# Spreading the closings, loads and weighings over the last stage of a two-layer graph-attention kernel

## The chip, the cores and the metric

The kernel runs on one core of one Trainium2 chip. The metric is the device time of one execution in microseconds (us), lower is better. The kernel before takes 3591.52 us, the median of three runs that lie between 3589.25 and 3591.77 us.

## The reference

The input `x` is 8 batches of 2048 nodes with 256 features; `adj` is one symmetric 2048 x 2048 adjacency matrix. Layer 0 is an attention with 4 heads of 64 features whose softmax runs over chunks of 256 keys, followed by two layer norms. Layer 1 is a graph attention with the same 4 heads:

```python
Wh = (h @ W).reshape(B, N, 4, 64)
e = s_src[:, :, None, :] + s_dst[:, None, :, :]      # per head
e = where(e > 0, e, 0.2 * e);  e = where(adj != 0, e, -inf)
alpha = softmax(e, axis=2)
h_out = elu(einsum('bijh,bjhd->bihd', alpha, Wh))
x = layernorm(x + h_out)                              # the output
```

The change touches layer 1 of the last batch, and what is done beside it, alone.

## The kernel before, in words

**Layer 1 in factored form.** The exponential of a sum is a product, so the weight of a pair of nodes is the maximum of a row value and a column value `gd`, masked, and the column's own factor `ed` is multiplied into the values beforehand. `waug` is the tile with the values of one batch: 128 partitions x 16 node tiles x 4 heads x 65 columns (64 values and the factor for the denominator). `factors(b, sd, waug)` makes these: its step `rows` stores the row factors to DRAM (`rowD`) and then has GpSimd (POOL in the profile) multiply `waug` by `ed` head by head, four `tensor_mul` in a row at line 767, the "weighing".

**Tiles and units.** Layer 1 of one batch is 8 units `(m, h)`: half `m` of the rows (1024 rows, 8 blocks of 128) and head `h`, in the order m=0 with h=0..3, then m=1 with h=0..3. A unit has 16 tiles, one for each block of 128 columns; all together are 128 tiles. One tile is one 128 x 1024 array `e` and then 32 small matmuls of TensorE (PE) at line 915 that accumulate `e` against `waug[:, j, h, :]` into the banks `pa`.

**The last stage stands alone.** Layer 1 of batch b is normally worked off beside layer 0 of batch b+1. The last batch, b = 7, has nothing beside it: `Layer1.alone` is true, and the program ends with a loop of 64 slots, two tiles each, so 8 slots make one unit. The order of instructions is written out by hand and every engine works through its own queue in that order; semaphores tie the queues together. In this stage

- VectorE (DVE) makes two tiles of three, at line 886, from a row `rowp` that ScalarE (ACT) has copied ("lifted") into PSUM at line 826;
- every third tile (`by_pool`) is made ahead by ACT (Relu and Identity, lines 855 and 856) and POOL (multiplication with the mask, line 857). `make_ahead` keeps four tiles (`LEAD`) ahead of the tile at hand;
- the row of a unit comes by four DMAs of the SP queue (`load_row`, posted in quarters, line 220 in the profile). It is asked for at tile 8 of the unit before (line 867) and lifted at tile 12 (line 879);
- the masks come as two tiles `et`, one for each half `m`, each by four DMAs of 512 KB (`load_masks`, line 799): the first before the stage, the second in `begin()` right ahead of it, into the buffer that the `waug` of batch 6 had;
- when a unit ends, ACT copies `pa` into `sums` (line 927), and a generator `close` finishes it in five steps, one step a slot (`rest(1)` in `step`): a denominator and its reciprocal `dn` on DVE (lines 940, 941), a multiplication on POOL (945), Exp and Relu on ACT (956, 957), and the sum into `h1` on DVE (959).

**Closings.** `Close` is the last layer norm of a group of 512 nodes. It loads `x1` of the group by four DMAs of 128 KB (`load`), adds it to `h1` on POOL (`pool`, line 997, 128 x 1024 elements), takes the statistics on DVE (`stats`, lines 540 to 549) with a power and a product on POOL (550, 551), and applies them on ACT (`finish`, line 588). The stores to the output follow with the next `send()`, on the SP queue as well. Tables say in which slot which group has which step: `CLOSING_ALONE` for the four groups of batch 6, `ENDING` for batch 7, whose groups 2 and 3 are finished after the loop. The slot's order is `send()`, then `lower.step()`, then the closings' steps.

Before the loop the remaining tiles of batch 6 are worked off; their DVE instructions read the row `srow` from SBUF, not from PSUM. The last tile of batch 6 and the first of batch 7 follow each other on PE without a barrier.

Of the kernel before, what the change touches and what calls it, by code (L numbers as in the profile page):

```python
# [10 lines left out]
F8 = mybir.dt.float8e4  # L11
# [6 lines left out]
P = 128  # L18
# [4 lines left out]
def adj_resnorm_kernel(  # L23
# [19 lines left out]
    nc = tc.nc  # L43
    B, N, F = x.shape
    H, D = a_src.shape
    NT = N // P
    NCH = N // CH
# [8 lines left out]
    QT = CH // P  # L56
# [15 lines left out]
    UNITS = [(m, h) for m in range(len(BANKS)) for h in range(H)]  # L72
# [4 lines left out]
    WIDE = max(BANKS)  # L77
    AHEAD_E = 5
    LEAD = 4
# [40 lines left out]
    qT = big.tile([P, KC, N], F32, tag="qT", name="qT")  # L120
    kT = big.tile([P, KC, N], F32, tag="kT", name="kT")
# [4 lines left out]
    edgeD = [tc.dram_tile([P, NT, n * P], F8, name=f"edgeD{m}") for m, n in enumerate(BANKS)]  # L126
# [79 lines left out]
    def send():  # L206
        while outgoing:
            outgoing.pop(0)()
# [4 lines left out]
    def drip(n=1):  # L213
        while pieces and n:
            pieces.pop(0)[1]()
            n -= 1
# [7 lines left out]
    def need(key):  # L224

        at = [k for k, piece in enumerate(pieces) if piece[0] == key]
        if at:
            drip(at[-1] + 1)
# [492 lines left out]
    def factors(b, sd, waug):  # L721

        s, d = sd[:, :H, :], sd[:, H:, :]
        top = small.tile([P, H], F32, tag="top", name="top")
        topb = top.unsqueeze(2).to_broadcast([P, H, NT])
        ed = small.tile([P, H, NT], F32, tag="ed", name="ed", bufs=1)
        gd = small.tile([P, H, NT], F32, tag="gd", name="gd")
        st = {}  # L730
        banks = one_bank if b + 1 < B else two_banks

        def most():
            nc.vector.tensor_reduce(top, d, AX.X, ALU.max)
            pt = banks([P, CH], "pt")
            nc.tensor.transpose(pt[:H, :P], top, identf)
            st["most"] = small.tile([H, 1], F32, tag="most", name="most")
            nc.vector.tensor_reduce(st["most"], pt[:H, :P], AX.X, ALU.max)

        def spread():  # L740
            pb = banks([P, CH], "pb")
            nc.tensor.matmul(
                pb[:, :H],
                lhsT=st["most"].to_broadcast([H, P]),
                rhs=identf[:H, :H],
                start=True,
                stop=True,
            )
            nc.vector.tensor_copy(top, pb[:, :H])
            nc.vector.tensor_add(s, s, topb)  # L750
            nc.vector.tensor_scalar(s, s, FAR, None, ALU.min)
            nc.scalar.activation(s, s, AF.Exp, scale=1.0 - SLOPE)
            nc.vector.tensor_sub(d, d, topb)
            nc.vector.tensor_scalar(d, d, -FAR, None, ALU.max)
            nc.scalar.activation(ed, d, AF.Exp)
            nc.scalar.activation(gd, d, AF.Exp, scale=SLOPE - 1.0)

        def rows():

            pr = banks([P, CH], "pr1")  # L760
            nc.tensor.transpose(pr[: H * NT, :P], s.rearrange("p h t -> p (h t)"), identf)
            flat = small.tile([H * NT, P], F32, tag="flat", name="flat", bufs=1)
            nc.scalar.copy(flat, pr[: H * NT, :P])
            nc.scalar.dma_start(out=rowD[b].rearrange("h (t p) -> (h t) p", p=P), in_=flat)
            nc.gpsimd.tensor_copy(waug[:, :, :, D], ed.rearrange("p h t -> p t h"))
            for h in range(H):
                nc.gpsimd.tensor_mul(
                    waug[:, :, h, :D],
                    waug[:, :, h, :D],
                    ed[:, h, :].unsqueeze(2).to_broadcast([P, NT, D]),  # L770
                )

        return gd, [most, spread, rows]


    class Layer1:
# [17 lines left out]
        def load_masks(self, m):  # L794

            pool, tag = ((big, "vaug"), (blocks, "waug"))[m]
            t = pool.tile([P, NT, WIDE * P], F8, tag=tag, name="et")
            for j in range(0, NT, QT):
                nc.sync.dma_start(out=t[:, j : j + QT, :], in_=edgeD[m][:, j : j + QT, :])
            self.masks[m] = t  # L800

        def start(self):
            self.load_row(0)
# [56 lines left out]
        def make(self):  # L860

            if self.made == TILES:
                return
            k = self.made
            n, j = k // NT, k % NT
            _, h = UNITS[n]
            if j == NT // 2:
                self.load_row(n + 1)
            self.made += 1
            if not self.alone:  # L870
                drip()
                if j == 0:
                    need(("row", self.b, n))
                self.load_edge(k + AHEAD_E)
                pool, tag = self.room
                e = pool.tile([P, WIDE * P], F32, tag=tag, name="e")
                row = self.rows[n]
            else:
                if j == NT - LEAD:
                    self.lift(n + 1)  # L880
                self.make_ahead(k)
                if self.by_pool(k):
                    return
                e = prp.tile([P, WIDE * P], F32, tag="pr", name="e")
                row = self.lifted[n]
            nc.vector.scalar_tensor_tensor(  # L886
                e,
                row,
                self.gd[:, h, j : j + 1],
                self.mask(k),  # L890
                op0=ALU.max,
                op1=ALU.mult,
            )
            self.e[k] = e
# [40 lines left out]
        def close(self, u, raw):  # L935
            m, h = UNITS[u]
            n = BANKS[m]

            dn = small.tile([P, n, 1], F32, tag="dn", name="dn")
            nc.vector.tensor_scalar(dn, raw[:, :, D:D1], 1e-30, None, ALU.max)  # L940
            nc.vector.reciprocal(dn, dn)
            yield 1
            if self.alone:
                v = raw[:, :, :D]
                nc.gpsimd.tensor_mul(v, v, dn.to_broadcast([P, n, D]))
            for k in range(n):
                if k == n // 2:
                    yield 1
                if not self.alone:
                    v = raw[:, k, :D]  # L950
                    nc.scalar.activation(v, v, AF.Copy, scale=dn[:, k, :])  # L951
            yield 1

            ee = small.tile([P, n, D], F32, tag="ee", name="ee")
            hp = raw[:, :, :D]
            nc.scalar.activation(ee, hp, AF.Exp)
            nc.scalar.activation(hp, hp, AF.Relu)
            yield 1
            nc.vector.scalar_tensor_tensor(
                h1[:, FIRST[m] : FIRST[m] + n, h * D : (h + 1) * D],  # L960
                ee,
                1.0,
                hp,
                op0=ALU.min,
                op1=ALU.add,
            )

        def step(self):
            self.rest(1)
            for _ in range(STEP):  # L970
                self.make()
                self.use()
# [117 lines left out]
    for g in range(NCH):  # L1090
# [36 lines left out]
        11: [(3, "factors"), (3, "finish")],  # L1127
    }
    CLOSING_ALONE = {
        -1: [(g, "load", kT, g) for g in range(NCH)],  # L1130
        1: [(0, "pool")],
        2: [(1, "pool")],
        3: [(0, "stats")],
        4: [(1, "stats")],
        5: [(0, "finish")],
        6: [(1, "finish")],
        8: [(2, "pool")],
        9: [(3, "pool")],
        10: [(2, "stats")],
        11: [(3, "stats")],  # L1140
        12: [(2, "finish")],
        13: [(3, "finish")],
    }
    ENDING = {
        30: [(g, "load", qT, g) for g in range(NCH)],
        37: [(0, "pool")],
        38: [(1, "pool")],
        39: [(0, "stats")],
        40: [(1, "stats")],
        41: [(0, "finish")],  # L1150
        42: [(1, "finish")],
        61: [(2, "most")],
        62: [(3, "most")],
    }
    lower = None
    for b in range(B):
        waug = blocks.tile([P, NT, H, D1], F32, tag="waug", name="waug")
        sd = small.tile([P, 2 * H, NT], F32, tag="sd", name="sd", bufs=1)
        closing = Closing(b - 2, CLOSING) if b > 1 else None
# [111 lines left out]
        send()  # L1271
        before = group
        gd, fs = factors(b, sd, waug)
        group = None

# [68 lines left out]
        lower = coming  # L1344
# [2 lines left out]
        lower.tail += undone  # L1347

    closing, ending = Closing(B - 2, CLOSING_ALONE), Closing(B - 1, ENDING)
    closing.do(-1, "load")  # L1350
    for _ in range(STEP):
        lower.make()
    for s in range(SLOTS):
        send()
        lower.step()
        for each in (closing, ending):
            each.do(s, "load", "pool", "stats", "most", "finish")
    send()
# [46 lines left out]
```

## Time and profile before

| what | value |
|---|---|
| median of three runs | 3591.52 us (3589.25 to 3591.77) |
| the profiled execution's own time | 3592.51 us |
| its span, from first to last instruction | 3590.6 us |
| busy over the span | PE 3512.4 us (98%), DVE 3040.5 (85%), ACT 2302.9 (64%), POOL 1424.7 (40%) |
| last stage, first to last tile on PE | about 3417.4 to 3577.3 us of the span |
| after the last tile | 13 us to the end of the span |

The profile is of one execution. "Busy" is the time in which an engine has an instruction under way; a wait is named by the engine that waits, the line, and what released it. PEclk is the share of TensorE's full clock that was granted. SPq is the queue of SyncE, which only issues DMAs. The last stage is 4.5% of the span, so the shares of the whole page say little of it; its own windows have to be asked for.

### The profile page before, as it was taken

The numbers are of one execution on the slowest core, as the hardware profiler recorded it, in microseconds if no ns is written. First come the engines' busy times: TensorE is split into PE (matmuls) and PEld (weight loads), VectorE is DVE, ScalarE is ACT, GpSimd is POOL, SyncE is SP. The second block draws the span as 40 slices with busy tenths as digits, with TensorE's granted clock in tenths as the row PEclk, the third lists the DMA queues.
The fourth block names the chain that finished last, engine by engine and source line by source line (L and its number), as shares of the span: only waits on it lengthen the run. The fifth ranks groups of instructions, "written<-read, shape, count | busy, mean of one in ns | idle before, by whom it ended". The sixth has DMA issues, their size and how long they took to land.

```text
span 3590.6 us, 170172 instructions
## 1 busy us (share of the span) xinstructions
PE 3512.4 (98%) x76892; PEld 2619.9 (73%) x76892; DVE 3040.5 (85%) x3655; ACT 2302.9 (64%) x4120; POOL 1424.7 (40%) x1255
## 2 busy tenths in 40 slices
PE   8999999999999999999999999999999999999787
PEld 5666677777777777776777767777677777777687
DVE  5886699977999699996999969998699987998787
ACT  5787556656666567665666657666576655666476
POOL 1555233333434333333443324334243333443366
PEclk9999999999999999999999999999999999999888
DMA  7663333443444444443444434444443443443341
GB/s 178 151 132 81 82 101 101 109 102 106 117 107 104 91 122 116 109 104 86 123 108 110 102 96 126 107 107 96 106 126 106 109 100 101 118 108 95 95 126 38
DMA packets 719848, 386.06 MB, mean 108 GB/s; under 512 B 433040, under 2 KB 679184, under 8 KB 719120
## 3 DMA queue, kind: packets, MB, share of 16 engines
q1 hardware_dynamic: 669120, 341.48, 38.0%
q10 hardware_dynamic: 50000, 33.70, 3.0%
q8 instruction: 601, 9.85, 1.2%
q14 instruction: 127, 1.04, 0.1%
HBM read 318.11 MB, written 56.89 MB: 104 GB/s over the span
## 4 chain that ended last, share of the span: by engine, by line
PE 86%; DVE 7%; issue 2%; DMA 2%; ACT 1%; POOL 1%; SPq 0%; DVEq 0%; ACTq 0%; POOLq 0%
PE pa L915 24%; PE pc L473 23%; PE ps L422 23%; PE pp L366 6%; PE po L625 3%; PE pv L382 3%; PE pw L667 3%; DVE e L886 3%; DVE pr L439 2%; POOL acc L499 1%; DMA et<-edgeD 1%; DVE h L439 0%; POOL part L497 0%; ACT e L855 0%; PE pm L270 0%
## 5 line engine op out<-in xcount | busy, mean ns | idle before, releaser
L462 ACT ACTIVATE pr<-pr 128x1024 f32<-128x1024 f32 x960 | 996.7, 1054 | 438.7 <-DVE pr L439 364.8
L439 DVE SCALAR_TENSOR_TENSOR pr<-ps,slab 128x1024 f32<-128x1024 f32 x960 | 1115.3, 1203 | 101.3 <-PE ps L422 83.6
L886 DVE SCALAR_TENSOR_TENSOR e<-srow,gd,et 128x1024 f32<-128x1024 f32 x896 | 1170.7, 1340 | 5.2
L915 PEld LDWEIGHTS pa<-waug,e 128*64 128x64 f32 x32768 | 1014.2, 140 | 213.4 <-issue 168.9
L915 PE MATMUL pa<-waug,e 128*64 128x65 f32 x32768 | 1066.6, 225 | 35.3 <-DVE e L886 30.7
L473 PE MATMUL pc<-vaug,pr 128*64 128x65 f32 x30720 | 980.8, 222 | 6.4 <-DVE pr L439 6.0
L497 POOL TENSOR_TENSOR part<-raw,rd 128x512 f32<-128x512 f32 x446 | 473.7, 1062 | 1221.3 <-DVE rd L490 1217.2
L473 PEld LDWEIGHTS pc<-vaug,pr 128*64 128x64 f32 x30720 | 938.0, 138 | 22.2 <-DVE pr L439 18.9
L422 PE MATMUL ps<-qT,kT 64*64 64x512 f32 x8192 | 942.3, 596 | 5.5 <-DVE pr L439 3.2
L422 PEld LDWEIGHTS ps<-qT,kT 64*64 64x64 f32 x8192 | 287.3, 132 | 482.5 <-issue 270.1
L480 ACT COPY raw<-pc 128x520 f32<-128x520 f32 x512 | 303.0, 592 | 492.7 <-PE pc L473 490.0
L499 POOL TENSOR_TENSOR acc<-acc,part 128x512 f32<-128x512 f32 x446 | 583.9, 1309 | 35.1
L490 DVE RECIPROCAL rd<-raw 128x8 f32<-128x8 f32 x512 | 100.4, 196 | 130.2 <-ACT raw L480 122.9
L497 POOL TENSOR_TENSOR acc<-raw,rd 128x512 f32<-128x512 f32 x64 | 66.8, 1044 | 361.1 <-DVE rd L490 361.1
L667 PE MATMUL pw<-w_sb,x1T 128*64 128x264 f32 (+1 forms) x800 | 124.4, 391 | 0.4 <-issue 0.2
L625 PE MATMUL po<-wo_sb,qT 128*64 128x256 f32 (+1 forms) x912 | 122.3, 384 | 0.1
L366 PE MATMUL pp<-xT,wk_sb 128*128 128x512 f32 x256 | 118.4, 603 | 2.9 <-DVE xT L322 1.6
L366 PE MATMUL pp<-xT,wq_sb 128*128 128x512 f32 x256 | 117.4, 598 | 0.0
L951 ACT ACTIVATE sums<-sums,dn 128x64 f32<-128x64 f32 x448 | 117.2, 334 | 0.0
L382 PE MATMUL pv<-wv_sb,xT 128*128 128x256 f32 x512 | 116.6, 381 | 0.0
L382 PEld LDWEIGHTS pv<-wv_sb,xT 128*128 128x128 f32 x512 | 95.9, 190 | 20.2 <-issue 7.2
L886 DVE SCALAR_TENSOR_TENSOR e<-rowp,gd,et 128x1024 f32<-128x1024 f32 x86 | 103.9, 1270 | 0.8 <-ACT rowp L826 0.8
(142 smaller groups left out, 2511.6 us busy)
## 6 DMA issues: line engine op xcount, KB each, us to landing
et<-edgeD SPq DMA_DIRECT2D x896, 128.0 KB, 2.8
slab<-clipD SPq DMA_DIRECT2D x256, 256.0 KB, 3.8
srow<-rowD SPq DMA_DIRECT2D x256, 128.0 KB, 3.6
xg<-in_x_dram SPq DMA_DIRECT2D x128, 128.0 KB, 3.3
x1D<-y ACTq DMA_DIRECT2D x32, 512.0 KB, 3.1
ctxD<-acc ACTq DMA_DIRECT2D x56, 256.0 KB, 3.6
ctx<-ctxD SPq DMA_DIRECT2D x224, 64.0 KB, 3.0
xp<-in_x_dram SPq DMA_DIRECT2D x224, 64.0 KB, 2.4
```

The source lines that it names most:

```text
L366: nc.tensor.matmul(pps[c], lhsT=w[:, kc, c * P : (c + 1) * P], rhs=st["xT"][:, kc, :], start=(kc == 0), stop=(kc == KC - 1),)
L382: nc.tensor.matmul(pv[:, u, :], lhsT=st["xT"][:, kc, u * P : (u + 1) * P], rhs=wv_sb[:, kc, :], start=(kc == 0), stop=(kc == KC - 1),)
L422: nc.tensor.matmul(ps[z * D : (z + 1) * D, k, :], lhsT=kT[rows, hp, t * P + z * D : t * P + (z + 1) * D], rhs=qT[rows, hp, cols], start=Tr ...
L439: nc.vector.scalar_tensor_tensor(pr, ps, -CLIP, row.unsqueeze(1).to_broadcast([P, 2, CH]), op0=ALU.max, op1=ALU.min,)
L462: nc.scalar.activation(pr, pr, AF.Exp, scale=0.125)
L473: nc.tensor.matmul(pc[z * D : (z + 1) * D, k, to], lhsT=probs[s][u][:, k, i * P + z * D : i * P + (z + 1) * D], rhs=vaug[:, KT * c + u, 2 ...
L480: nc.scalar.copy(raws[s].rearrange("p k i d -> p k (i d)"), pc[:, :, : QT * D1])
L497: engine.tensor_mul(part, raw[:, :, :, :D], rd.to_broadcast([P, 2, QT, D]))
L499: engine.tensor_add(accv, accv, part)
L667: nc.tensor.matmul(pw[z, k, : F + 2 * H], lhsT=self.x1T[:, c, u * P + z.start : u * P + z.stop], rhs=w1_sb[:, c, :], start=(c == 0), stop= ...
L886: nc.vector.scalar_tensor_tensor(e, row, self.gd[:, h, j : j + 1], self.mask(k), op0=ALU.max, op1=ALU.mult,)
L915: nc.tensor.matmul(self.pa[i // QT][z * D : (z + 1) * D, i % QT, :], lhsT=e[:, i * P + z * D : i * P + (z + 1) * D], rhs=self.waug[:, j, h ...
```

## The change

In layer 1 of the last batch:

- the weighing of heads 1, 2 and 3 is taken out of `rows` and done in slots 1, 5 and 9 of the loop; head 0 is still weighed in `rows`;
- the second mask's four DMAs move from `begin()` to slots 15, 17, 19 and 21, one in each;
- a unit's row is asked for at tile 1 of the unit before in place of tile 8, and lifted at tile 8 in place of tile 12;
- `x1` of a group of batch 6 is loaded in slots 0, 2, 9 and 12 in place of all four ahead of the loop; for batch 7 in slots 34, 36, 45 and 47 in place of all at 30;
- the steps of the closings lie further apart: `pool` of batch 6 in slots 4, 6, 16, 18 (before 1, 2, 8, 9), `stats` in 8, 10, 20, 22 (3, 4, 10, 11), `finish` in 11, 13, 23, 25 (5, 6, 12, 13); for batch 7 `pool` in 40, 42 (37, 38), `stats` in 44, 46 (39, 40), `finish` in 47, 49 (41, 42);
- `close` of the first six units of this stage has one empty step ahead of `dn` and one ahead of the last sum, so seven steps in place of five; `step` takes two steps when more than one closing is waiting.

```diff
-            for h in range(H):
-                nc.gpsimd.tensor_mul(
-                    waug[:, :, h, :D],
-                    waug[:, :, h, :D],
-                    ed[:, h, :].unsqueeze(2).to_broadcast([P, NT, D]),
-                )
-
-        return gd, [most, spread, rows]
+            for h in range(H if b + 1 < B else 1):
+                weigh(h)
+
+        def weigh(h):
+            nc.gpsimd.tensor_mul(
+                waug[:, :, h, :D],
+                waug[:, :, h, :D],
+                ed[:, h, :].unsqueeze(2).to_broadcast([P, NT, D]),
+            )
+
+        return gd, [most, spread, rows, weigh]
...
-            t = pool.tile([P, NT, WIDE * P], F8, tag=tag, name="et")
-            for j in range(0, NT, QT):
-                nc.sync.dma_start(out=t[:, j : j + QT, :], in_=edgeD[m][:, j : j + QT, :])
-            self.masks[m] = t
+            self.masks[m] = pool.tile([P, NT, WIDE * P], F8, tag=tag, name="et")
+            if m == 0:
+                for k in range(QT):
+                    self.load_part(m, k)
+
+        def load_part(self, m, k):
+            js = slice(k * NT // QT, (k + 1) * NT // QT)
+            nc.sync.dma_start(out=self.masks[m][:, js, :], in_=edgeD[m][:, js, :])
...
-            if j == NT // 2:
+            if j == (1 if self.alone else NT // 2):
                 self.load_row(n + 1)
...
-                if j == NT - LEAD:
+                if j == NT // 2:
                     self.lift(n + 1)
...
+            wide = self.alone and u < len(UNITS) - 2
+            if wide:
+                yield 1
             dn = small.tile([P, n, 1], F32, tag="dn", name="dn")
...
             yield 1
+            if wide:
+                yield 1
             nc.vector.scalar_tensor_tensor(
...
-            self.rest(1)
+            self.rest(1 + (len(self.tail) > 1))
...
-        -1: [(g, "load", kT, g) for g in range(NCH)],
-        1: [(0, "pool")],
-        2: [(1, "pool")],
-        3: [(0, "stats")],
...
+        0: [(0, "load", kT, 0)],
+        2: [(1, "load", kT, 1)],
+        4: [(0, "pool")],
+        6: [(1, "pool")],
+        8: [(0, "stats")],
+        9: [(2, "load", kT, 2)],
...
-    closing.do(-1, "load")
+    weigh = fs[3]
     for _ in range(STEP):
         lower.make()
     for s in range(SLOTS):
         send()
         lower.step()
+        if s % QT == 1 and s // QT + 1 < H:
+            weigh(s // QT + 1)
+        if s % 2 and 14 < s < 14 + 2 * QT:
+            lower.load_part(1, (s - 14) // 2)
         for each in (closing, ending):
             each.do(s, "load", "pool", "stats", "most", "finish")
```

More of the change, by code (lines that the diff above doesn't have):

```diff
@@ L1129, in adj_resnorm_kernel @@
     CLOSING_ALONE = {
-        -1: [(g, "load", kT, g) for g in range(NCH)],
-        1: [(0, "pool")],
-        2: [(1, "pool")],
-        3: [(0, "stats")],
[L1134 to L1142, printed above, removed]
+        0: [(0, "load", kT, 0)],
[4 more added lines that the diff above has]
+        9: [(2, "load", kT, 2)],
+        10: [(1, "stats")],
+        11: [(0, "finish")],
+        12: [(3, "load", kT, 3)],
+        13: [(1, "finish")],
+        16: [(2, "pool")],
+        18: [(3, "pool")],
+        20: [(2, "stats")],
+        22: [(3, "stats")],
+        23: [(2, "finish")],
+        25: [(3, "finish")],
     }
     ENDING = {
[L1145 to L1151, printed above, removed]
+        34: [(0, "load", qT, 0)],
+        36: [(1, "load", qT, 1)],
+        40: [(0, "pool")],
+        42: [(1, "pool")],
+        44: [(0, "stats")],
+        45: [(2, "load", qT, 2)],
+        46: [(1, "stats")],
+        47: [(0, "finish"), (3, "load", qT, 3)],
+        49: [(1, "finish")],
         61: [(2, "most")],
```

## The prediction, written before the changed kernel was run

> **What bounds the kernel now.** I read the chain of work that ended last, then windows of the last stage, then waits and queues inside it. The page's chain:
>
> ```profile
> PE 86%; DVE 7%; issue 2%; DMA 2%; ACT 1%; POOL 1%; SPq 0%; DVEq 0%; ACTq 0%; POOLq 0%
> ```
>
> Over the span TensorE is the bound, but nothing before about 3397 us is touched. So I cut the end into windows: first the tail of batch 6, then the eight units, each ending where ACT begins to copy the unit's `sums` (line 927). Columns: stretch, length, busy time of PE, PEld, DVE, ACT, POOL, granted TensorE clock, DMA share, GB/s.
>
> ```profile
> 3398.70:3417.35 18.65, 13.21 (x262) 12.37 (x257) 18.33 (x10) 1.39 (x2) 10.08 (x4) 0.63 0.17 52
> 3417.35:3446.05 28.70, 20.83 (x542) 20.49 (x544) 18.98 (x33) 23.68 (x35) 19.47 (x12) 0.82 0.61 199
> 3446.05:3469.93 23.88, 18.15 (x497) 17.59 (x494) 22.49 (x34) 17.84 (x25) 18.96 (x13) 0.86 0.27 81
> 3469.93:3487.00 17.07, 15.91 (x546) 15.77 (x542) 14.97 (x14) 15.92 (x18) 12.58 (x7) 1.00 0.27 81
> 3487.00:3503.37 16.37, 14.89 (x494) 14.53 (x490) 14.28 (x13) 14.03 (x17) 12.34 (x8) 1.00 0.47 138
> 3503.37:3518.86 15.49, 14.90 (x504) 14.62 (x500) 14.05 (x14) 13.82 (x15) 10.42 (x7) 1.00 0.02 5
> 3518.86:3543.45 24.59, 19.38 (x584) 19.24 (x580) 20.06 (x34) 20.18 (x26) 19.41 (x13) 0.86 0.31 88
> 3543.45:3560.92 17.47, 15.06 (x454) 14.78 (x452) 14.28 (x13) 13.91 (x17) 11.82 (x8) 0.90 0.02 4
> 3560.92:3577.30 16.38, 15.79 (x528) 15.38 (x522) 13.03 (x13) 8.59 (x10) 11.86 (x7) 1.00 0.02 4
> ```
>
> Five units take 15.5 to 17.5 us (mean 16.56) and three 28.7, 23.9 and 24.6. These three hold the closings; together they stand 27.5 us above three ordinary ones. In them no engine is busy all the time: they wait for each other, and TensorE falls to 0.82 to 0.86 of its clock. The waits in the stage:
>
> ```profile
> PE pa L915 <- DVE e L886: 20.7, 10, 5.2
> DVE dn L940 <- ACT sums L927: 15.2, 7, 3.4
> DVE st_c L540 <- POOL h L997: 9.2, 2, 6.7
> ACT rowp L826 <- DMA srow<-rowD: 5.5, 2, 4.7
> ```
>
> PE waits for DVE, and DVE stands in its queue for other things: a reciprocal whose copy isn't made, statistics whose sum POOL hasn't done. ACT's lift waits for a row that is late because of SP's order:
>
> ```profile
> 3417.41 1.75 SPq L799 DMA_DIRECT2D et<-edgeD  x4
> 3419.20 12.67 SPq L220 DMA_DIRECT2D kT<-x1D  x16
> 3431.97 1.80 SPq L220 DMA_DIRECT2D srow<-rowD  x4
> ```
>
> The row leaves 14.6 us after the mask, and ACT lifts it at 3436.70. In the tail of batch 6, DVE takes 16.29 us for eight tiles from 3398.36; POOL weighs from 3397.75 for 11.03 us. The instructions by line, with min/median/max in ns:
>
> ```profile
> L886 DVE SCALAR_TENSOR_TENSOR e<-srow,gd,et x896: 1228/1277/2945, 400.5 to 3413.4; 128x1024 f32<-128x1024 f32 x180
> L886 DVE SCALAR_TENSOR_TENSOR e<-rowp,gd,et x86: 1231/1273/1284, 3414.6 to 3573.7; 128x1024 f32<-128x1024 f32 x86
> ```
>
> ```profile
> L767 POOL TENSOR_TENSOR waug<-waug,ed x32: 1902/1924/2906, 389.3 to 3405.9; 128x1024 f32<-128x1024 f32 x32
> ```
>
> Beside a weighing the form with `srow` rises to 2.9 us and the weighing from 1.92 to a mean of 2.79; the form with `rowp` never exceeds 1.28 beside any POOL work.
>
> **What the Trainium skill says.** "SBUF — State Buffer", section "Who interferes with whom": a VectorE instruction with two SBUF inputs contends with a GpSimd instruction that reads SBUF; one with at most one SBUF input, outside the two-port modes, does not. The three rows above agree: `srow` and `et` are two SBUF inputs, `rowp` is in PSUM. "TensorE: Matmul & The Clock Gate", Part 1: activity releases a throttle of the array and idleness brings it back. The windows agree: 1.00 in most ordinary units, 0.63 in the tail of batch 6.
>
> **The change, part by part.** T0 is the end of batch 6's last tile on PE, now 3417.4.
>
> *Weighing off the tail.* Three of four weighings go. Four of the eight DVE tiles are slow now, (16.29 − 8 × 1.21) / 4 = 1.65 us each, 1.21 being the start-to-start step of undisturbed tiles. One slow tile stays: DVE ends 5.0 us earlier, at 3409.7 in place of 3414.7. PE follows within one tile if its clock holds, for it is then fed every 1.21 us and now idles 5.4 us in four gaps. Between 5 and 6.5 us; I take **6**, T0 = 3411.4. ACT's lift of row 0 ends at 3406.2, before that.
>
> *Units 0 to 3.* The weighings cost POOL 3 × 1.92 = 5.8 us here, DVE reading PSUM. POOL's queue in order, with e at 2.02, a closing's sum 2.37, power and product 1.2, a unit's multiplication 1.04: the tile numbers are e2, e5, e8, weigh 1, e11, e14, sum, e17, weigh 2, sum, e20, e23, power, weigh 3, multiplication, e26, power, e29, e32. ACT leads to e14: two copies, five pairs at 2.22, batch 6's last closing (2.0 + 1.27), and the lift (1.0, now unwaited), T0 + 15.6 by the trace's own 14.5 plus the lift. So e14 leaves POOL at T0 + 17.6 and unit 0 ends near T0 + 20 (28.7 now). From there POOL leads: 2 sums, 2 weighings, 6 e, 2 powers, 1 multiplication = 4.74 + 3.84 + 12.1 + 2.4 + 1.04 = 24.1, so tile 32 starts near T0 + 41.7 (52.6 now). Units 2 and 3: POOL has 2 sums, 2 powers, 2 multiplications and 10 to 11 e, 31 us; ACT 11 pairs, 2 lifts, 2 copies, 2 closings of units, 2 finishes = 24.4 + 2.0 + 1.3 + 2.5 + 4.1 = 34.3. ACT leads: T0 + 76 (86.0 now). That is **10** us.
>
> *Units 4 to 7.* Unit 5 has sums in slots 40 and 42 and powers after 44 and 46: POOL 10.8 + 1.04 + 4.74 + 2.4 = 19.0, taken as 19.5 (24.6 now). Unit 6 gets a finish of 2.1 on ACT, 18.0 (17.5 now); units 4 and 7 about 16 each. 69.9 against 73.9: **4** us.
>
> *Costed at nothing.* The row's four DMAs go earlier; SP needs 1.8 us for them and ACT lifts seven tiles later, against 3.4 us to landing. Waiting in SP for the old row's last reader, they hold back x1, masks and stores behind them; that reader ran tiles before. Mask 2 is issued from slot 15 on and read first from slot 30: 15 us for 6.4 to landing. x1 in slots 0, 2, 9, 12 has four slots or more ahead of its sum, against 3.9 to landing. Stores precede the next row in slots 24 and 48; the lift is four slots later. If this cover fails, a lift waits, and DVE and PE behind it: the 4.7 us of now is the bound. The empty steps add no instruction; ahead of `dn` they give DVE work while ACT copies. The 15.2 us there are mostly not on the path, since in ordinary units PE is 86 to 96% busy: 0 to 1 us a unit, nothing taken. `h1` of unit 0 comes in slot 14, after the last finish that reads it (13); `sums` is free one slot before its next copy. After the last tile nothing changes.
>
> *Sum.* 6 + 10 + 4 = 20, less 2.5 because queues never run without gaps and PE, starved some 4 us ahead of tile 20, loses clock: **17.5 us**. The profiled execution takes 3592.5 (span 3590.6 and 1.9 around it), 1.0 above the median: 3592.5 − 17.5 − 1.0 = **3574**.
>
> **Unknown costs.** Weighing beside the new instructions was never seen: 1.92 as the best, 2.79 each as the worst, between 0 and 2.6 us. That the sum of three gains is only bunching undone: at best all 27.5 us and 6.5 go, less the 5.8 of weighing: 28. At worst the closings cost what they cost now wherever they stand: 6 alone.
>
> **Rivals.**
>
> *B, everything hides* (0.14): the waits vanish wholly, 28 us, 3563. Against: POOL's 24.1 us for tiles 17 to 32.
>
> *C, the weighing waits* (0.08): if a weighing counts as writing all of `waug`, POOL waits for PE to finish earlier tiles and PE for the weighing, three times about 3.5 us (1.92 and an e behind it, 2.02, less the overlap). 17.5 − 10.5 gives 7: 3584.5. No row of before shows either way.
>
> *F, only the tail gains* (0.05): closings cost what they cost, 6 us, 3586. Against: DVE's 6.7 us wait for the sum and ACT's 4.7 for the row are order, not work.
>
> *D, slower* (0.09): POOL becomes the bound and PE's clock stays down. In unit 1 POOL has two sums and two weighings ahead of tiles that PE waits for. In the tail of batch 6, with gaps of 0.9 to 2.5 us, the clock fell to 0.63 and a tile took 2.0 us. If units 0 to 2 ran at 1.9 us a tile, 48 tiles take 91 us in place of 69.7: 21 lost, 10 gained, 3602. It decides from 80 us, or 1.66 us a tile. Against: units 0 and 1 with 1.6 now hold worse gaps and keep 0.82.
>
> The forecast (0.64) covers 3566 to 3583. Within 0.2%, 7.2 us, about what a measurement can tell from no change, lie F and half of C. **Faster 0.82, same 0.09, slower 0.09.** The range 3562 to 3587 takes in B, C and F and leaves D out.
>
> **What would show it.** Right: one DVE tile above 2 us in the tail and T0 near 3411; units 0 and 1 near 20 and 22 us, unit 5 near 19.5; no wait of statistics for POOL's sum, none of `rowp` for a DMA; POOL weighing near 1.92. Wrong: PE waiting for POOL's e by more than 8 us in units 0 to 2, weighings preceded by waits for PE, a clock under 0.7 there, or units 0 to 3 above 86 us.

## The result, and the profile after

The changed kernel takes 3578.56 us, the median of six runs (3576.38 to 3582.95), where the kernel before took 3591.64 (3587.53 to 3593.22, six runs with those of the first table). The ratio is 0.9969, with a 95% interval from 0.9959 to 0.9979: faster by 13 us, or 0.31%. The forecast was 3574 with a range of 3562 to 3587. The direction and the range hold; the gain is 13 where 17.5 was forecast.

The profiled execution took 3576.82 us, its span is 3575.0. The chain of work that ended last breaks off inside the last stage in this trace, so its line says nothing:

```profile
PE 0%; ACT 0%; DVE 0%; issue 0%; POOL 0%; ACTq 0%; POOLq 0%; DVEq 0%
```

So I cut the stage as before. The windows of the kernel after, first the tail of batch 6 from 1.9 us after the POOL copy at line 765, then the eight units from one copy of `sums` to the next (the border of tail and unit 0 in the windows of before, 3417.35, lay 0.45 us behind that copy; the table below has one cut for all); columns as before (length, busy PE, PEld, DVE, ACT, POOL, clock, DMA share, GB/s):

```profile
3395.90:3407.63 11.73, 9.20 (x254) 8.89 (x250) 11.73 (x9) 1.02 (x1) 1.49 (x1) 0.85 0.30 81
3407.63:3430.39 22.76, 16.18 (x522) 15.62 (x518) 17.69 (x17) 20.21 (x28) 16.53 (x9) 1.00 0.40 119
3430.39:3453.89 23.50, 17.85 (x534) 17.18 (x531) 23.40 (x34) 18.14 (x24) 21.07 (x14) 0.93 0.30 89
3453.89:3473.68 19.79, 16.73 (x506) 16.38 (x502) 19.61 (x35) 16.23 (x18) 16.70 (x10) 0.91 0.43 139
3473.68:3491.61 17.93, 15.91 (x534) 15.63 (x531) 15.01 (x15) 17.64 (x23) 12.72 (x9) 1.00 0.38 120
3491.61:3507.66 16.05, 14.88 (x503) 14.66 (x501) 15.05 (x13) 13.71 (x16) 13.11 (x8) 1.00 0.38 103
3507.66:3526.59 18.93, 16.03 (x527) 15.46 (x522) 17.88 (x32) 16.12 (x17) 15.65 (x11) 1.00 0.21 59
3526.59:3544.34 17.75, 15.50 (x510) 15.16 (x512) 16.34 (x15) 17.55 (x24) 14.01 (x9) 1.00 0.19 64
3544.34:3561.60 17.26, 15.63 (x522) 15.22 (x517) 14.23 (x13) 8.52 (x11) 13.05 (x8) 1.00 0.02 4
```

Three things are to be seen: the tail is far shorter and at a higher clock; units 0 and 5 fell, from 28.7 and 24.6 us to 22.8 and 18.9; and unit 1 did not fall at all (23.5 against 23.9), with DVE busy 23.40 of 23.50 us. To compare all kernels I use one cut: the tail from the start of the POOL copy at line 765 to the start of ACT's copy of `sums`, then each unit from copy to copy, the last one to DVE's first instruction after it. In us, from the traces:

```
                 tail  unit 0    1      2      3      4      5      6      7    all   0 to 3
before          20.11  29.15  23.88  17.07  16.37  15.49  24.59  17.47  16.40  180.5   86.5
changed         13.64  22.76  23.50  19.79  17.93  16.05  18.93  17.75  17.38  167.7   84.0
weigh_only      13.75  28.67  25.09  17.04  16.96  15.49  24.37  16.97  16.41  174.8   87.8
all_but_weigh   18.75  21.74  21.83  18.25  18.72  16.03  20.48  17.74  17.37  170.9   80.5
closings_only   19.89  22.14  20.19  19.21  19.95  15.56  19.40  20.05  19.32  175.7   81.5
rows_masks_only 18.74  26.49  24.03  17.82  16.55  15.60  23.62  15.91  16.40  175.2   84.9
stats_on_pool   13.64  22.30  26.14  18.70  17.93  17.11  20.72  17.74  17.38  171.7   85.1
both_ports      13.64  22.32  26.11  18.73  17.94  15.66  20.95  17.73  15.94  169.0   85.1
late_sum        13.64  20.36  27.11  20.30  17.93  16.40  20.53  17.73  18.88  172.9   85.7
two_weighs_out  13.64  22.66  21.29  18.25  18.52  16.62  20.50  17.74  18.95  168.2   80.7
later_weighs    13.64  22.20  21.58  19.03  17.99  15.51  18.91  17.79  17.38  164.0   80.8
sum_slot_15     13.75  22.42  24.06  20.11  17.98  15.85  20.94  17.78  18.95  171.8   84.6
later_stats     13.64  21.90  22.61  20.19  17.93  15.02  20.95  17.73  18.95  168.9   82.6
later_late      13.75  20.36  21.99  19.12  17.94  16.35  18.90  17.74  17.37  163.5   79.4
```

Each line is one execution. Units 4 to 7 have the same instructions in the changed kernel, all_but_weigh, late_sum, two_weighs_out, later_weighs, sum_slot_15 and later_late, and still unit 5 is 18.9 or 20.5 to 20.9, unit 7 is 17.4 or 18.9, and the four together are 69.6 to 73.8 us. So a difference below 2 us in one unit, or below some 4 us in the sum of four, says nothing if it stands in one pair of traces alone. In the traces the stage gained 12.8 us: 6.5 in the tail, 2.5 in units 0 to 3, 3.8 in units 4 to 7. The span fell by 15.6 because this execution also reached line 765 2.8 us sooner, in a part that the change doesn't touch.

The waits of the stage, after (us in total, times, longest):

```profile
PE pa L922 <- DVE e L893: 10.8, 6, 3.1
PE pa L922 <- POOL e L864: 9.0, 6, 2.4
DVE h L971 <- ACT sums L967: 6.8, 2, 5.0
DVE dn L950 <- ACT sums L934: 5.1, 3, 2.1
```

PE's waits for DVE halved (20.7 before) and its waits for POOL's tiles rose (2.6 before). DVE's waits for POOL's sum and ACT's for a row are gone, and a new one stands there: DVE waits for ACT's Relu (line 967) before the sum into `h1` (line 971), 5.0 us of it in unit 0. SP's queue in the timeline (start, length, queue and line, transfer, count) shows why the row is in time: it leaves at 3406.87, ahead of `x1` and before unit 0 begins at 3407.63.

```profile
3406.87 2.16 SPq L220 DMA_DIRECT2D srow<-rowD  x4
3409.07 3.75 SPq L220 DMA_DIRECT2D kT<-x1D  x8
```

In the tail one DVE tile of eight is slow (min/median/max in ns), and of the four weighings only the one in the tail is longer than 1.93 us; the other three run beside tiles with `rowp` in PSUM:

```profile
L893 DVE SCALAR_TENSOR_TENSOR e<-srow,gd,et x8: 1271/1271/2919, 3395.6 to 3405.6; 128x1024 f32<-128x1024 f32 x8
```

```profile
L770 POOL TENSOR_TENSOR waug<-waug,ed x4: 1920/1926/2450, 3394.9 to 3439.5; 128x1024 f32<-128x1024 f32 x4
```

### The profile page after: what moved, and what is told of

It is laid out like the page before. It is cut to its first block, busy times and chain, and to the rows that moved or that the text cites. A ratio compares the mean times of both kernels' runs of the same rounds, so it can differ in the third digit from the quotient of the medians.

```text
span 3575.0 us, 170176 instructions
## 1 busy us (share of the span) xinstructions
PE 3500.7 (98%) x76892; PEld 2608.3 (73%) x76892; DVE 3041.6 (85%) x3655; ACT 2301.9 (64%) x4120; POOL 1422.8 (40%) x1255
## 5 line engine op out<-in xcount | busy, mean ns | idle before, releaser
L439 DVE SCALAR_TENSOR_TENSOR pr<-ps,slab 128x1024 f32<-128x1024 f32 x960 | 1115.6, 1204 | 100.3 <-PE ps L422 82.6
L922 PEld LDWEIGHTS pa<-waug,e 128*64 128x64 f32 x32768 | 1002.6, 139 | 210.9 <-issue 173.3
L922 PE MATMUL pa<-waug,e 128*64 128x65 f32 x32768 | 1055.1, 223 | 32.3 <-DVE e L893 17.5
L473 PEld LDWEIGHTS pc<-vaug,pr 128*64 128x64 f32 x30720 | 937.9, 138 | 21.8 <-DVE pr L439 18.9
```

Of the source, the lines that this page charges most:

```text
L439: nc.vector.scalar_tensor_tensor(pr, ps, -CLIP, row.unsqueeze(1).to_broadcast([P, 2, CH]), op0=ALU.max, op1=ALU.min,)
L473: nc.tensor.matmul(pc[z * D : (z + 1) * D, k, to], lhsT=probs[s][u][:, k, i * P + z * D : i * P + (z + 1) * D], rhs=vaug[:, KT * c + u, 2 ...
L922: nc.tensor.matmul(self.pa[i // QT][z * D : (z + 1) * D, i % QT, :], lhsT=e[:, i * P + z * D : i * P + (z + 1) * D], rhs=self.waug[:, j, h ...
```

## The experiments

All ratios are to the kernel before, of runs on the same chip. First the parts of the change, each by itself.

**weigh_only**: the kernel before with `weigh` split off and, in the loop,

```diff
+        if s % QT == 1 and s // QT + 1 < H:
+            weigh(s // QT + 1)
```

> The kernel before, with the weighing of heads 1 to 3 moved to slots 1, 5 and 9 and nothing else. Theory (the tail's gain is the weighing's alone): the tail of batch 6 shortens by 6.5 us as in the full change (20.1 to 13.6 us from the copy at line 765 to the copy of sums). The three weighings then stand among the bunched closings of unit 0 and 1: the POOL queue theory wants units 0 and 1 longer by their 5.8 us, total 0 to -2 us; if POOL has room there (it is busy 19.5 of 28.7 us), units 0 and 1 stay within 2 us and the total is -5 to -6.5 us.

Measured: 3586.8 us, ratio 0.9984 (0.9977 to 0.9991). The tail is 13.75 us, units 0 and 1 are 53.8 against 53.0, the stage is 5.8 shorter. So the tail's gain is the weighing's alone, and where the other queues stand waiting POOL had room for the weighings, as the second of the two expectations has it.

**all_but_weigh**: the changed kernel with the weighing back in `rows`.

```diff
-            for h in range(H if b + 1 < B else 1):
+            for h in range(H):
```

> The changed kernel with all four weighings back in the rows step. Theory: the tail stays at 20.1 us (+6.5 against the change). Units 0 to 3 lose 5.8 us of POOL work: if POOL's queue leads there, 84.0 falls to about 78; if VectorE's small instructions that wait for POOL lead, it falls by 2 to 4 us, since fewer POOL instructions stand in their way; if neither, it stays at 84. Total against before: -6 to -12 us.

Measured: 3580.7 us, ratio 0.9968 (0.9956 to 0.9981). Units 0 to 3 are 80.5 us, 3.4 below the change: of what the tail gains, 3.4 us are paid back there. By the expectation this is the size of the ports' theory (2 to 4 us), not of POOL's whole queue (6 us). The times don't show the rest of the gain: the ratio is 0.9968 here and 0.9969 in the full change. The tail was 18.75 us, 1.4 below 20.11, and so it was in rows_masks_only: in these two traces the first weighing (1.90 us) falls on the sum into `h1`, which takes 2.44 us in place of 0.68, and only three DVE tiles are slow, not four. In all these traces that weighing and that sum start within 0.02 us of each other, and no run shows what decides. So what the weighing costs the tail is 5.0 to 6.5 us, and the 6.5 are the upper end.

**closings_only**: the kernel before with the two tables, the empty steps and `rest(1 + (len(self.tail) > 1))`.

> The kernel before with the closings' tables, the empty steps and the second step alone (x1 loaded group by group with them); rows at tile 8, lifts at tile 12, second mask ahead of the loop, weighing in one piece. Theory: unit 5 falls from 24.6 to about 19 us as in the full change, units 0 to 3 fall from 86.5 by 2 to 5 us, tail unchanged. Total -7 to -10 us. Rival (unit 5 owes its gain to the earlier row): unit 5 stays above 22 us.

Measured: 3586.6 us, ratio 0.9988 (0.9982 to 0.9995). Unit 5 is 19.4 us, so it owes its gain to the spread closings; units 0 to 3 fall by 5.0. But the total fell by 5.3 us where 7 to 10 were expected, since units 6 and 7 are 2.6 and 2.9 us longer than before and units 4 to 7 together gain nothing (74.3 against 73.9): the stage has three waits of `rowp` for its row, 5.1 us together, two of them in units 3 and 6 behind the closings' stores, and DVE waits 5.6 us for `rowp`. The spread needs the earlier rows: this part and rows_masks_only gain 5.3 and 2.3 us by themselves and 11.2 together (all_but_weigh).

**rows_masks_only**: the kernel before with

```diff
-            if j == NT // 2:
+            if j == (1 if self.alone else NT // 2):
...
-                if j == NT - LEAD:
+                if j == NT // 2:
```

and the second mask in slots 15 to 21.

> The kernel before with rows asked for at tile 1, lifted at tile 8, and the second mask in slots 15 to 21, nothing else. Theory: ACT's 4.7 us wait for the row of unit 1 goes, but VectorE's wait of 6.7 us for POOL's sum of the closing stays, so unit 0 falls by 0 to 4 us; unit 5 falls by at most 2. Total -1 to -5 us. Rival (rows are what the change gains by): units 0 to 3 fall by over 5 us and unit 5 by 5.

Measured: 3589.65 us, ratio 0.9992 (0.9985 to 0.9998). Unit 0 falls by 2.7 us, unit 5 by 1.0; in the stage ACT no longer waits for a row, while DVE still waits 7.6 us for POOL's sums. As the first theory has it, not the rival.

Next, why units 0 to 3 gained so little. Unit 1 has DVE full. Its queue there, in the changed kernel:

```profile
3430.86 1.39 DVE L540 BATCH_NORM_STATS2 st_c<-h 128x6 f32<-128x256 f32 x4
3432.17 0.36 DVE L543 BATCH_NORM_AGGREGATE mv_c<-st_c 128x2 f32<-128x6 f32 x4
3432.56 1.79 DVE L548 TENSOR_SCALAR rs_c<-mv_c 128x4 f32<-128x4 f32 x1
3434.27 2.05 DVE L549 TENSOR_SCALAR off_c<-mv_c 128x4 f32<-128x4 f32 x1
3436.24 2.05 DVE L950 TENSOR_SCALAR dn<-sums 128x8 f32<-128x8 f32 x1
```

Three instructions on 4 or 8 elements a partition take 5.9 us, where the same take 0.15 to 0.17 elsewhere in the trace; a POOL instruction is under way all that time, and each of the three ends within 0.04 us of the end of one. POOL's queue there:

```profile
3431.94 2.39 POOL L1009 TENSOR_TENSOR h<-h,kT 128x1024 f32<-128x1024 f32 x1
3434.28 3.97 POOL L864 TENSOR_TENSOR e<-e,et 128x1024 f32<-128x1024 f32 x2
```

With `rs` of the next closing (1.90) and the sum `h` (1.10 for 0.68) some 7.6 us of unit 1 are such stretching. So my first theory was **ports**: VectorE's time is what its small instructions lose beside POOL. The rivals were **POOL's queue**, which makes what the others need too late, and, for unit 0, the **new wait** for ACT's Relu.

**stats_on_pool**: the changed kernel with

```diff
-                nc.vector.tensor_scalar(self.rs, self.mv[:, :, 1], EPS, None, ALU.add)
-                nc.vector.tensor_scalar(self.off, self.mv[:, :, 0], -1.0, None, ALU.mult)
+                small_ops = nc.gpsimd if self.name == "c" else nc.vector
+                small_ops.tensor_scalar(self.rs, self.mv[:, :, 1], EPS, None, ALU.add)
+                small_ops.tensor_scalar(self.off, self.mv[:, :, 0], -1.0, None, ALU.mult)
```

> The changed kernel with the two small VectorE instructions of each closing's statistics (rs and off, 128 x 4) given to POOL; everything else as changed. In the changed kernel these twelve took 10.7 us in the loop where 0.17 each would make 2.0, because they wait for a POOL instruction to end. Theory (VectorE is held by ports in unit 1, where it was busy 23.4 of 23.5 us): unit 1 falls from 23.5 by 4 to 6 us, since 5.4 us of the waits of rs and off stand in it; total -4 to -7 against the change. Rival (POOL's queue leads): POOL gets two more instructions of 0.2 us per closing, so units 0 to 3 stay at 84 or lengthen by 1 us.

Measured: 3584.72 us, ratio 0.9977 (0.9968 to 0.9985). Unit 1 is 26.1 us. The stretching of `rs` and `off` is gone, and DVE stands 5.8 us in unit 1 for another reason: unit 0's sum into `h1` may not overwrite what ACT's finish of group 1 is still reading, and that finish comes behind POOL's second power. I call this wait the gate:

```profile
DVE h L972 <- ACT kT L589: 5.8, 1, 5.8
```

To take the stretching away wins nothing. The test isn't a clean one, since the two instructions now stand in POOL's queue.

**both_ports**: also the denominators' maximum read from PSUM.

```diff
+                for i, pa in enumerate(pas):
+                    nc.vector.tensor_scalar(
+                        dn[:, i * QT : (i + 1) * QT, :], pa[:, :, D:D1], 1e-30, None, ALU.max
+                    )
```

> As the one before, and also the denominators' maximum (dn, line 950) read from the PSUM banks in place of the SBUF copy, two instructions of 128 x 4 in place of one of 128 x 8. Theory of ports: a PSUM source can't be held by POOL, so each of the two takes 0.16 us in place of a mean of 0.955; another 5 to 6 us of VectorE's time in eight units goes; total -5 to -10 against the change. Rival (POOL's queue leads): no change in units 0 to 3 beyond 1 us, at most 1 us in all.

Measured: 3582.63 us, ratio 0.9972 (0.9960 to 0.9984); units 0 to 3 are 85.1 us, as in stats_on_pool. The maximum takes 0.16 us now and puts nothing on POOL, and VectorE waits the longer at the gate (7.5 us): no gain from a second relief of the same kind.

**late_sum**: batch 6's last closing gets two empty steps ahead of its sum.

```diff
+            late = self.b == B - 2 and u == len(UNITS) - 1
...
+            if late:
+                yield 1
+                yield 1
```

> The changed kernel with two empty steps ahead of the last sum of batch 6's last unit, so that it comes in slot 6 in place of slot 4. In the changed kernel VectorE waited 5.0 us for it in unit 0 (line 971 for ACT's Relu). Theory: that wait goes and unit 0 falls from 22.8 by 2 to 4 us; the rest stays; total -2 to -4. Rival (unit 0 is led by ACT and POOL, who make every third tile): VectorE only waits elsewhere, unit 0 falls by less than 1 us.

Measured: 3583.4 us, ratio 0.9971 (0.9959 to 0.9982). Unit 0 falls by 2.4 us to 20.4, so the wait cost that; unit 1 takes 3.6 back, and of the expected gain in all (2 to 4 us) nothing is seen. What unit 1 waits for is in DVE's queue of this kernel, the gate again:

```profile
3452.22 2.16 DVE L975 SCALAR_TENSOR_TENSOR h<-ee,sums 128x512 f32<-128x512 f32 x1 [4.75 <-ACT kT L588]
```

**two_weighs_out**: the weighing of heads 2 and 3 is left out.

> The changed kernel without the weighing of heads 2 and 3 (left out, so that their output differs). It takes 2 x 1.92 = 3.8 us of POOL out of slots 5 and 9. Theory of POOL's queue: units 0 to 3 fall by 3.5 to 4 us, all of it in units 0 and 1. Theory of ports: they fall by 1 to 3 us, less than POOL's time, since VectorE's small instructions meet fewer POOL instructions but still meet some.

Measured: 3581.43 us, ratio 0.9967 (0.9954 to 0.9979). Units 0 and 1 fall from 46.3 to 44.0 us, units 0 to 3 by 3.3: between the two expectations, nearer to POOL's queue.

**sum_slot_15**: one more empty step ahead of unit 0's sum.

```diff
+            if wide and u == 0:
+                yield 1
```

> The changed kernel with one more empty step ahead of unit 0's sum, which so comes in slot 15 in place of 14; POOL's queue is as it was. Theory of the gate: VectorE makes one or two more tiles before it stands at the sum, so unit 1 falls by 1 to 2.5 us (23.5 to 21 to 22.5). Rival (POOL's tiles lead unit 1 by themselves): unit 1 stays within 1 us of 23.5, and PE's waits move from VectorE to POOL.

Measured: 3580.77 us, ratio 0.9970 (0.9960 to 0.9981). Unit 1 is 24.1 us. The sum stands clear of the finish (it starts at 3452.41, the finish ended at 3449.42) and nothing is won; ACT's next copy of `sums` waits 2.7 us for the sum instead. But in the changed kernel's trace, too, the sum has no wait for the finish, so there was none to win back. Unit 1 stays within 1 us, as the rival has it, but PE's waits didn't move to POOL: in unit 1 they are 4.4 us for DVE and 2.2 for POOL. A later sum alone doesn't help.

**later_weighs**: the weighings of heads 2 and 3 go behind the bunch.

```diff
-        if s % QT == 1 and s // QT + 1 < H:
-            weigh(s // QT + 1)
+        if s in (1, 13, 21):
+            weigh(1 + (s > 1) + (s > 13))
```

> The changed kernel with the weighing of heads 2 and 3 in slots 13 and 21 in place of 5 and 9; head 1 stays in slot 1. Theory (the gate): in units 0 and 1 POOL's queue makes the second closing's power late, ACT's finish of group 1 follows it, and unit 0's sum on VectorE may not overwrite h1 before that finish has read it, so the queue of VectorE's tiles stands behind it (41.5 us after the stage's start). With 3.8 us of POOL work taken from ahead of that power, the sum comes at about 38 to 39.5 us and units 0 and 1 fall from 46.3 to 43 to 44 us, as with two weighings left out (43.95); units 2 and 3 take 0 to 2 us back, as POOL had spare time there. Total -1 to -3 us against the change. Rival (POOL's sum of work counts, not its place): the 3.8 us come back wholly in units 1 and 2, units 0 to 3 stay within 1 us of 84.

Measured: 3575.99 us, ratio 0.9963 (0.9950 to 0.9977). Units 0 and 1 fall to 43.8 us, units 2 and 3 keep 37.0 (37.7 in the change), units 0 to 3 are 80.8. The sum comes 39.5 us into the stage, at the end of what was expected, still with a wait of 1.3 us for the finish. In this trace the same POOL work costs nothing at another place in its queue, against the rival, that only the amount counts; the times alone (0.9963 against 0.9969) don't tell the two kernels apart.

**later_stats**: later_weighs and stats_on_pool together.

> The weighings in slots 1, 13 and 21, and the statistics' two small instructions on POOL in place of VectorE. If POOL's queue was the one limit and VectorE's waits for ports the next one behind it, units 1 and 2 fall below those of the later weighings alone (21.6 and 19.0), together by 2 to 4 us. If POOL's queue is still the limit, its four instructions of 0.23 us more per pair of closings make units 0 to 3 0 to 2 us longer than 80.8.

Measured: 3579.93 us, ratio 0.9970 (0.9959 to 0.9981); units 0 to 3 are 82.6 us, 1.8 longer than with the later weighings alone and not shorter by 2 to 4. Even with the queue relieved, nothing is won by taking the stretched instructions off DVE; whether it costs something is within the noise.

**later_late**: later_weighs and late_sum together.

> The weighings in slots 1, 13 and 21, and batch 6's last sum in slot 6 in place of 4. If POOL's queue no longer stands in the way, the 2.4 us that unit 0 fell by with the late sum stay won: unit 0 at about 20, units 0 to 3 at 78.5. If it still does, unit 1 gives them back, units 0 to 3 at 80 to 82.

Measured: 3574.57 us, ratio 0.9957 (0.9945 to 0.9970), the lowest of all; its interval and that of the changed kernel still overlap, and the two were only compared through the kernel before. Units 0 and 1 in its windows:

```profile
3409.24:3429.60 20.36, 16.53 (x537) 15.98 (x533) 18.26 (x17) 20.00 (x28) 14.13 (x7) 1.00 0.38 115
3429.60:3451.59 21.99, 16.45 (x518) 15.48 (x516) 17.96 (x33) 17.81 (x25) 21.83 (x15) 1.00 0.37 114
```

Units 0 to 3 are 79.4 us, between the two expectations. Unit 0 keeps what the late sum won, and in unit 1 POOL is busy 21.83 of 21.99 us while DVE stands 4 us, 3.8 of them at the gate: there it is POOL's queue that is full.

Three pairs of kernels differ in the place of two weighings alone: the change and later_weighs, stats_on_pool and later_stats, late_sum and later_late. From the first of a pair to the second units 0 to 3 fall by 3.2, 2.4 and 6.3 us, and the ratio falls by 0.0006, 0.0007 and 0.0014. No pair is clear of the noise by its times; all three go the same way. Against the ports speaks the second pair, where VectorE's stretching in units 0 to 3 is alike, 6.9 us in both (its small `tensor_scalar` counted above 0.16 us each and the sums above 0.68).

## Why the prediction was right, and where it was off

*Weighing off the tail* (6 forecast): 6.5 measured, of a range of 5.0 to 6.5 that the traces of before and its like leave open. One slow tile is left of four, DVE's eight tiles take 11.29 us in place of 16.29, and weigh_only shows that it is the weighing's doing. The price of 1.92 us for a weighing beside `rowp` holds.

*Units 4 to 7* (4 forecast; the parts written there, 16, 19.5, 18 and 16, make 69.5 and not 69.9): 3.8 measured, unit 5 at 18.9 against 19.5. That it fits so well is partly luck: the seven traces with the same instructions gain 0.1 to 4.4 us, 2.2 in the mean. closings_only gives unit 5's gain to the spread closings.

*Units 0 to 3* (10 forecast): 2.5 measured; this is the term that was mis-sized, 84.0 us in place of 76. Three steps of it failed.

Unit 0 was to take 20 us and took 22.8. The forecast counted the work of batch 6's last closing on ACT, but not that this closing keeps its five steps, so that DVE stands at its sum in slot 4 while ACT reaches the Relu ahead of it late: DVE waits 5.0 us. Before, DVE was held at that point by POOL's sum (6.7 us), so the new wait was hidden behind the one that went. late_sum gives 20.4.

"Tile 32 starts near T0 + 41.7" failed though its ledger was right: POOL finishes e29 and e32 in this line of the changed kernel, at 3449.70, which is 42.1 us after the copy that starts unit 0.

```profile
3445.70 4.00 POOL L864 TENSOR_TENSOR e<-e,et 128x1024 f32<-128x1024 f32 x2
```

But unit 2 starts only at 46.3, since a tile being ready is not a tile reached: in unit 1 PE waits 3.8 us for DVE's tiles and 1.8 for POOL's, and DVE is busy 23.40 of 23.50 us. POOL's dense queue sets DVE back in two ways: by the small instructions that stretch beside it (7.6 us of unit 1 in the changed kernel), and by the gate, where the second power holds up ACT's finish and the finish, over `h1`, unit 0's sum. In the changed kernel the second way is just covered by the first; the finish ends at 3448.44, and DVE comes to the sum 0.7 us later:

```profile
3446.38 2.06 ACT L588 ACTIVATE kT<-h,off_c,rs_c 128x256 f32<-128x256 f32 x4
3449.14 1.10 DVE L971 SCALAR_TENSOR_TENSOR h<-ee,sums 128x512 f32<-128x512 f32 x1
```

That sum I had costed at nothing because slot 14 comes after slot 13; but slots are an order and not a time, and the finish of slot 13 ended 40.8 us into the stage. The two ends lie so close that taking away one of them (stats_on_pool, both_ports, sum_slot_15) wins nothing, while taking two or three weighings from ahead of both on POOL takes 3.2 to 3.4 us off units 0 to 3 (two_weighs_out, later_weighs, all_but_weigh). The traces part cleanly by this. In the five kernels with weighings in slots 1, 5 and 9 (the change, sum_slot_15, stats_on_pool, both_ports, late_sum) that finish ends 40.2 to 41.4 us after the start of unit 0, and units 0 and 1 take 46.3 to 48.4 us. In the five where two or three of them are later, left out or back in the tail, it ends at 37.8 to 39.6, and the two units take 42.4 to 44.5. Thus the forecast named the right queue for unit 1, POOL's, and left out what hangs on it.

Units 2 and 3 were to take 34.3 us by ACT's ledger and took 37.7. I made none for DVE, and in unit 2 it is busy 19.61 of 19.79 us: beside its tiles it has the statistics of two closings, one instruction of them stretched to 1.08 us, and a sum into `h1` of 1.52. No run separated this further; in all kernels with the spread closings these two units take 36.6 to 39.2 us, and what holds them there stays open.

*Costed at nothing.* Rows, second mask and `x1` held: no wait of `rowp` for a DMA is left in the stage. closings_only shows what the earlier rows cover: 5.1 us of lifts.

*The deduction of 2.5 us* for gaps and a lost clock took back, by luck, a third of the 7.5 us by which that term was too large. The clock, 0.91 to 1.00 in all units, isn't what fills unit 1, where PE is busy 17.85 of 23.50 us.

*Rivals.* B (all hides) is refuted: PE still waits 19.8 us in the stage for DVE's and POOL's tiles. C (weighing waits for PE) doesn't occur: none of the weighings has a wait ahead of it in the trace. F (only the tail gains) is refuted by all_but_weigh, which gains 11.2 us with all four weighings in the tail. D (slower) named the right place, POOL in unit 1, but a unit there took 1.47 us a tile and not 1.66, and the clock stayed at 0.93. Of the signs of being wrong, PE waiting more than 8 us for POOL's tiles in units 0 to 2 came to 4.2.

The Trainium skill's "SBUF — State Buffer", section "Who interferes with whom", which I used for the tail, says as well that `tensor_scalar` can run in a two-port mode, in which it needs the port pair that VectorE shares with GpSimd and is blocked wholly while a GpSimd instruction holds it. Unit 1 agrees: 0.16 us became 1.8 to 2.05 three times, with POOL busy. The prediction named the exception of the two-port modes and put no cost on it.

## What to carry to other kernels

Spread work by the queue that it stands in, not by slots: when one in-order engine is full over a stretch, ask what else is released by an instruction deep in its queue, and move work that isn't due yet behind that instruction (here two weighings, by 8 and 12 slots, worth about 3 us in the traces and not resolved by the times of one pair of kernels). A ledger of one engine gives the time at which its work is ready, not the time at which it is used; make it for each engine that feeds the same consumer, tiny instructions at their stretched price included. And where a wait is taken away, name the instruction behind it that then waits first.

## What the runs showed of the hardware

In this case's traces VectorE's `tensor_scalar` on 128 x 4 or 128 x 8 elements in SBUF takes 0.15 to 0.17 us undisturbed and up to 2.4 us beside POOL; in unit 1 the stretched ones end within 0.04 us of the end of a POOL instruction. The reciprocal on 128 x 8 stays at 0.20 us and the maximum from PSUM at 0.16 (both_ports). A POOL `tensor_scalar` on 128 x 4 takes 0.23 us (stats_on_pool). That moving such instructions off VectorE didn't make the kernel faster, though some were stretched more than tenfold, I had not expected.

In the tail of the kernel before, a DVE tile with two inputs in SBUF and a weighing take turns. The four weighings end at 3400.20, 3403.07, 3405.92 and 3408.78, the four slow tiles at 3401.28, 3404.14, 3407.00 and 3409.86: every tile ends 1.1 us after a weighing, and every next weighing 1.8 us after a tile. So both look long (2.9 us each), but a pair takes 2.86 us, about what the two take one after the other: they don't overlap.
